# Turning a column vector with VectorE and storing it from ScalarE's queue, in place of a TensorE transpose

## The chip, the core and the metric

The kernel runs on one core of a Trainium2 chip. A core has TensorE (PE: matrix products, and transposes as products with an identity), VectorE (DVE), ScalarE (ACT), GpSimd (POOL) and SyncE (SP), which run side by side and wait for each other through semaphores. DMAs are started by instructions of SP, ACT or POOL and run on 16 DMA engines of the core. The metric is the device time of one execution in microseconds (us). The kernel before took 1218.98 us (median of 3 runs, 1218.74 to 1221.97).

## The reference

Sixteen graphs of 1024 nodes with 256 features go through two layers. `adj` holds only zeros and ones. Cut to what matters:

```python
# layer 0: gated sum over neighbours
e0    = leaky(einsum('bid,bjd->bij', h * a0, h))          # slope 0.2
alpha = sigmoid(where(adj == 1, e0, -max))                # 0 where there is no edge
x     = layernorm(x + einsum('bij,bjd->bid', alpha, h) + bias)
# layer 1: graph attention
Hh    = x @ W
s, d  = Hh @ a[:256], Hh @ a[256:]
e     = where(adj != 0, exp(-leaky(s[:, None] + d[None, :])), 0)
x     = layernorm(x + elu((e @ Hh) / rowsum(e)))
```

Since exp(-leaky(z)) is the smaller of exp(-z) and exp(-0.2 z), the kernel writes it as exp(-0.2 z) times min(1, p q), where p belongs to the row node (from s) and q to the column node (from d). The row's own factor falls out in the division by the row sum, and the column's factor is multiplied into H. What is left of `e` for an edge is min(p q, 1), and for no edge min(p q, 0): one VectorE instruction, min(p q, adj).

## The kernel before, in words

All work is float32. The nodes of one graph are cut into 8 tiles of 128. The main loop runs over b = 1 to 15, and I call one turn a slot. A slot makes layer 0 of graph b and layer 1 of graph b-1 ("prev"), and ends the layer norm of graph b-2 ("done"). A 16th part behind the loop makes layer 1 of the last graph. The order of all instructions is the order of the Python text, engine by engine (`manual_schedule`). Each engine takes its instructions strictly in that order.

A slot starts with the eight score strips jt = 0 to 7 (`strip`, L240): TensorE multiplies (L254) into PSUM tiles, ScalarE takes two tanh (L262, L263), VectorE the larger of them (L264), `finish` (L266) masks it with adj, and POOL adds 2 to the diagonal (`add_twice`, L284). The scores are symmetric, so a strip is made only right of the diagonal. What lies under it is a turned copy: `dump` (L286) turns the strip in squares of 32x32 on VectorE (L290) and stores it in DRAM in four pieces from SP's queue (L294), and `gather` (L296) loads it back into `al` with one DMA (L298). `mask` (L302) then masks it on VectorE (L305). I write dump 3, gather 1 and so on for the strip that they belong to. On SP's queue the order around the change is dump 2, gather 1, dump 3, gather 2, gather 3, dump 4, dump 5, gather 4.

The product of alpha and x is made of seven smaller ones (`product`, L457, and `combine_al`, L449, whose VectorE instructions are L455). Layer 1 of prev runs between: `project` (L567) makes H, and ScalarE writes p into columns 0 to 7 and q into columns 8 to 15 of the tile `pq_kept`, 128 partitions x 32 columns (L594), one column a node tile. After all eight, `share_p` (L606) brings p, which lies down the partitions, into a row that every partition has: the tile `p`, 128 x 1024. `weights` (L637) reads it in L643, and `sum1` (L647) multiplies the result with H (L648).

In `share_p` TensorE turns `pq_kept` (L610) into PSUM, ScalarE copies the 8 x 128 result to the tile `row` (L612), POOL stores it in DRAM as `p_row` (L614, eight rows of 512 bytes), and, when that has landed, loads it back onto all partitions (L616). Only then does POOL go on to `center` (L368) of graph done: L338, L357 to L363, L373 and L374, small instructions on 128 x 8 elements that give the scale of the layer norm. ScalarE's `scale1` (L379) waits for it, and on ScalarE's queue `check_adj` (L130) and `unite(b, "c11")` (L499) stand behind `scale1`. VectorE's `turn_y(b, 1)` (L521) waits for L499, and `weights` 5 to 7 stand behind that.

In the last slot `share_half` (L618) does the same work for half of p at a time and in another way: VectorE turns the whole `pq_kept` in squares of 32x32 (L624). Then p of node tile t lies in row t of each of the four blocks of 32 partitions, and four DMAs from POOL's queue, one a block, store it (L628).

One thing that the text does not show is in the built program. The DMAs of SP and of ACT share eight completion semaphores, given in turn in the order of the program. A DMA waits, before it is issued, until the DMA eight places before it has landed, unless other waits ensure that already. POOL's DMAs have semaphores of their own.

Of the kernel before, what the change touches and what calls it, by code (L numbers as in the profile page):

```python
# [9 lines left out]
F32 = mybir.dt.float32  # L10
# [8 lines left out]
P = 128  # L19
HALF = 512  # L20
BIG = 1.0e30
SLOPE = 0.2
SQ = 32
# [7 lines left out]
def one_kind_pass(  # L31
# [33 lines left out]
    nc = tc.nc  # L65
    B, N, D = x.shape
    NT = N // P
    ND = D // P
    HT = HALF // P
# [6 lines left out]
    one = ctx.enter_context(tc.tile_pool(name="one", bufs=1))  # L76
    two = ctx.enter_context(tc.tile_pool(name="two", bufs=2))
    dram = ctx.enter_context(tc.tile_pool(name="dram", bufs=2, space=bass.MemoryType.DRAM))
    small = ctx.enter_context(tc.tile_pool(name="small", bufs=3))
    ps_e = ctx.enter_context(tc.tile_pool(name="ps_e", bufs=3, space=PSUM))  # L80
    ps_t = ctx.enter_context(tc.tile_pool(name="ps_t", bufs=2, space=PSUM))
# [27 lines left out]
    def adj_rows(b, j0, j1, columns):  # L109

        for g in range(2):
            k0, k1 = max(j0, g * HT), min(j1, (g + 1) * HT)
            if k0 < k1:
                yield slice(k0, k1), adjs[b, g][:, k0 - g * HT : k1 - g * HT, columns]
# [35 lines left out]
    ident = const.tile([P, P], F32, tag="ident", name="ident")  # L150
# [29 lines left out]
    pq_kept = const.tile([P, SQ], F32, tag="pq", name="pq_kept")  # L180
# [121 lines left out]
    def mask(b, t, j0=0, j1=NT):  # L302
        for js, rows in adj_rows(b, max(t + 1, j0), j1, ts(t, P)):
            v = als[b][:, js, ts(t, P)]
            nc.vector.scalar_tensor_tensor(v, v, 1.0, rows, ALU.add, ALU.mult)  # L305
# [143 lines left out]
    def combine_al(b, k, j0, j1):  # L449

        left, right = slice(0, HALF), slice(HALF, N)
        top, low = als[b][:, j0:j1, :], als[b][:, HT + j0 : HT + j1, :]
        t1, m12, m21, m22 = top[:, :, left], top[:, :, right], low[:, :, left], low[:, :, right]
        out_, in0, in1 = {1: (t1, t1, m12), 2: (t1, m21, t1), 3: (m12, t1, m12), 4: (m21, m22, t1)}[k]
        nc.vector.tensor_tensor(out_, in0, in1, ALU.subtract)  # L455

    def product(b, k):  # L457

        left, right = slice(0, HALF), slice(HALF, N)
        top, low = als[b][:, 0:HT, :], als[b][:, HT:, :]  # L460
        x_ = xs[b]
        lhs, rhs = {
            1: (x_[:, 0:HT, 0:P], top[:, :, right]),
            2: (x_[:, HT:, 0:P], low[:, :, right]),
            3: (Ss[b][:, 2, :, :], low[:, :, left]),
            4: (x_[:, HT:, P:D], low[:, :, left]),
            5: (Ss[b][:, 0, :, :], top[:, :, left]),
            6: (Ss[b][:, 1, :, :], top[:, :, left]),
            7: (x_[:, 0:HT, P:D], top[:, :, right]),
        }[k]  # L470
        bank = {1: "Q", 2: "Q", 3: "V", 5: "V", 4: "W", 7: "W", 6: "R"}[k]
        first = k in (1, 5, 6, 7)
        if first:
            pool, tag = {"Q": (ps_t, "t"), "V": (ps_acc, "acc")}.get(bank, (ps_e, "e"))
            banks[bank] = pool.tile([P, HALF], F32, tag=tag, name=f"p{bank}_{b}")
        for jt in range(HT):
            nc.tensor.matmul(  # L477
                banks[bank],
                lhsT=lhs[:, jt, :],
                rhs=rhs[:, jt, :],  # L480
                start=first and jt == 0,
                stop=jt == HT - 1,
                skip_group_check=True,
            )
# [27 lines left out]
    def new_yT(b):  # L512
        yTs[b] = x1Ts[b] = one.tile([P, ND, N], F32, tag="x1T", name=f"yT_{b}")
# [24 lines left out]
    x1Ts, Hs, pqs, p_bcs, es = {}, {}, {}, {}, {}  # L538
# [64 lines left out]
            nc.scalar.mul(H, acc, wr)  # L603
        unscaled.clear()

    def share_p(b):  # L606


        pt = ps_t.tile([P, HT, P], F32, tag="t", name=f"prow_{b}")[0:NT, 0, :]
        nc.tensor.transpose(pt, pq_kept[:, 0:NT], ident)  # L610
        row = one.tile([NT, P], F32, tag="row", name=f"row_{b}")
        nc.scalar.copy(row, pt)  # L612
        p_row = dram.tile([N], F32, tag="p_row", name=f"p_row_{b}")
        nc.gpsimd.dma_start(p_row.rearrange("(t p) -> t p", p=P), row)  # L614
        p_bcs[b] = one.tile([P, N], F32, tag="p", name=f"p_{b}")
        nc.gpsimd.dma_start(p_bcs[b], p_row.partition_broadcast(P))  # L616

    def share_half(b, t0):  # L618


        if t0 == 0:
            p_bcs[b] = one.tile([P, N], F32, tag="p", name=f"p_{b}")
        pT = one.tile([P, SQ], F32, tag="pT", name=f"pT_{b}_{t0}")
        nc.vector.transpose(pT, pq_kept)  # L624
        p_row = dram.tile([HALF], F32, tag="p_half", name=f"p_row_{b}_{t0}")
        v = p_row.rearrange("(t i j) -> i t j", i=P // SQ, j=SQ)
        for i in range(P // SQ):
            nc.gpsimd.dma_start(v[i], pT[ds(i * SQ + t0, HT), :])  # L628
        nc.gpsimd.dma_start(p_bcs[b][:, ds(t0 * P, HALF)], p_row.partition_broadcast(P))

    def check_pq(b):
        near = small.tile([P, 2, NT], F32, tag="near", name=f"near_{b}")
# [80 lines left out]
    def deviation1(b, t):  # L713
        deviation(ys[b][t], mv1s[b][:, t, :])
# [66 lines left out]
    for b in range(1, B):  # L781
        prev, done = b - 1, b - 2
# [6 lines left out]
        for jt in range(NT):  # L789
            if jt == 4:  # L790
                mask(b, 0, 0, HT)
                combine_al(b, 1, 0, 2)
            if jt == 5:
                new_yT(b)
                product(b, 1)
                share_p(prev)
                mask(b, 1, 0, HT)
                combine_al(b, 1, 2, 3)
                mask(b, 0, HT)
                mask(b, 1, HT)  # L800
                mask(b, 2, 0, HT)
                combine_al(b, 1, 3, HT)
                mask(b, 2, HT)
                if done >= 0:
                    r1s[done] = center(mv1s[done], f"1_{done}", unit=1.0 / D)
            if jt == 6:
                unite(b, "p1")
                product(b, 5)
                unite(b, "p5")
                combine_al(b, 2, 0, HT)  # L810
            strip(b, jt)
            if jt == 5:
                mask(b, 3, HT)
            finish(b, jt, ends=False)
            if jt == 4:
                gather(b, 3)
            if jt < NT - 1:
                dump(b, jt)
            if jt < 2 and done >= 0:
                deviation1(done, NT - 2 + jt)  # L820
            if prev == 0 and jt == 0:
                turn_x1(0, 0)
            if prev == 0 and jt == 1:
                transpose_x1(0)
            if jt >= 1 and jt != 4:
                gather(b, jt - 1)
            if jt < 4 and b == 1:
                combine_x(b, jt)
            for t in projects[jt]:
                project(prev, t)  # L830
            if jt == 4:
                evict_H()
            add_twice(b, jt)
# [74 lines left out]
        for t in range(NT):  # L908
            if t >= n_first:
                acc = sum_of(t)  # L910
                for m in range(NT):
                    sum1(prev, t, acc, m)
            if last and t == 7:
                for m in range(4):
                    weights(b, m, 0, HT)
            elu(prev, t, *((first[t], rinvs[t]) if t < n_first else (acc,)))
            if last and t in (2, 3):
                for q in range(HT):
                    stats0(b, (t - 2) * HT + q)
                roots0(b, t - 2)  # L920
            if t >= 1:
                add(prev, t - 1)
            if t >= 2:
                deviation1(prev, t - 2)
            if not last and t in (3, 5):
                sums0(b, (t - 3) // 2)
                if t == 5:
                    load_adj(b + 1, 1, behind=mv0s[b][:, HT, 0:1])
            if not last and t >= 4:
                for q in range(2 * t - 8, 2 * t - 6):  # L930
                    deviation0(b, q)
                if t % 2 == 1:
                    roots0(b, (t - 5) // 2)
            for n in ([0], [1], [2, 3])[t - 5] if not last and t >= 5 else []:
                combine_x(b + 1, n)
            if t == 3 and not last:
                scale_x(b + 1, 0)
                scale_x(b + 1, 1)
            if last and t in (4, 6):
                t0 = (t - 4) // 2 * HT  # L940
                for n in range(HT):
                    project(b, t0 + n)
                evict_H()
                share_half(b, t0)
            if last and t in (5, 7):
                for q in range(HT):
                    scale0(b, (t - 5) // 2 * HT + q)
            if last and t == 7:
                for m in range(4, 6):
                    weights(b, m, 0, HT)  # L950
# [524 lines left out]
```

## Time and profile before

The profiled execution took 1218.96 us, and its span was 1217.2 us (1.76 us lie outside). TensorE's granted clock was 0.998.

| | busy us | share of the span |
|---|---|---|
| TensorE | 1206.9 | 99% |
| VectorE | 993.4 | 82% |
| ScalarE | 846.5 | 70% |
| GpSimd | 391.2 | 32% |
| the 15 transposes of L610, as listed | 15 x 0.273 = 4.1 | 0.3% |
| the 15 copies of L612 | 15 x 0.255 = 3.8 | 0.3% |
| POOL's wait for `p_row` to land (L616) | 40.5 in 15 | 3.3% |

A slot starts with the first product of its strip 0; these starts are at 130.42, 204.84, 279.26, 353.68, 428.10, 502.52, 577.14, 651.56, 726.17, 800.59, 875.87, 950.29, 1024.71 and 1099.43 us in the chain of waits. Their distance is 74.42 us, and longer in the slots from 502.52 (74.62), 651.56 (74.61), 800.59 (75.28) and 1024.71 (74.72). "At +22.4" below means 22.4 us after the start of a slot.

How to read the profile: a line of the timeline has the start in us, the length in us, the engine (SPq is SP's DMA queue), the line of the kernel, the operation, output<-inputs, sizes and the count of merged instructions. In brackets stand the idle time of the engine just before and what ended it. "DMA al<-mir" there means that a DMA landed.

### The profile page before, as it was taken

The page shows a single profiled execution, that of the slowest core. Times are in us where ns is not written, and L with a number is a line of the kernel's source. Part 1 is how long each engine was busy: PE and PEld are TensorE (multiplying, and loading weights), DVE is VectorE, ACT ScalarE, POOL GpSimd, SP SyncE. Part 2 cuts the span into 40 slices and gives each one's busy share as a digit, 9 for nine tenths or more (in the row PEclk, how much of TensorE's full clock was granted, in tenths as well). Part 3 has the DMA queues.
Part 4 walks back from the last instruction along what each step waited for, and adds up shares of the span by engine and source line. Part 5 has one row for each costly group of instructions (what it writes and reads, how often), then busy time and mean ns, then how long its engine had stood idle before and what let it go on. Part 6 is the DMA issues. An engine that isn't in the chain of part 4 may idle for free.

```text
span 1217.2 us, 15868 instructions
## 1 busy us (share of the span) xinstructions
PE 1206.9 (99%) x4400; PEld 819.4 (67%) x4400; DVE 993.4 (82%) x1759; ACT 846.5 (70%) x2150; POOL 391.2 (32%) x730
## 2 busy tenths in 40 slices
PE   9999999999999999999999999999999999999997
PEld 6757657576575866758667585775757657576686
DVE  5698797887969789797897978879798796887957
ACT  4574867767687676867768677786776867577674
POOL 3320333404243142441414324143340433404243
PEclk9999999999999999999999999999999999999999
DMA  9568787797878878788787886877769787887512
GB/s 195 104 133 153 130 158 154 148 184 137 154 152 155 180 136 160 145 166 172 142 171 132 156 179 132 176 139 143 173 143 189 128 156 151 156 182 137 112 52 73
DMA packets 604600, 180.66 MB, mean 148 GB/s; under 512 B 482012, under 2 KB 586968, under 8 KB 604504
## 3 DMA queue, kind: packets, MB, share of 16 engines
q1 hardware_dynamic: 582800, 136.90, 56.0%
q0 software_dynamic: 21008, 42.01, 18.8%
q8 instruction: 37, 0.61, 0.2%
q10 hardware_dynamic: 696, 0.66, 0.2%
q14 instruction: 59, 0.48, 0.1%
HBM read 152.44 MB, written 60.62 MB: 175 GB/s over the span
## 4 chain that ended last, share of the span: by engine, by line
PE 96%; ACT 2%; DVE 1%; POOL 1%; DMA 0%; issue 0%; ACTq 0%; DVEq 0%; POOLq 0%
PE acc L648 36%; PE pe L254 20%; PE pH L582 9%; PE pQ L477 8%; PE pV L477 8%; PE pW L477 8%; PE pR L477 4%; PE acc L396 2%; ACT junk L130 0%; ACT y_kept L379 0%; DMA p_row<-row 0%; PE busy L149 0%; PE pal L313 0%; ACT x L379 0%; POOL ve L338 0%
## 5 line engine op out<-in xcount | busy, mean ns | idle before, releaser
L648 PE MATMUL acc<-H,e 128*128 128x257 f32 x2032 | 445.6, 380 | 0.6 <-DVE e L643 0.6
L648 PEld LDWEIGHTS acc<-H,e 128*128 128x128 f32 x2032 | 384.8, 190 | 64.8 <-issue 7.2
L254 PE MATMUL pe<-xa,xT 128*128 128x384 f32 (+1 forms) x720 | 249.5, 486 | 0.2 <-DVE xa L235 0.2
L254 PEld LDWEIGHTS pe<-xa,xT 128*128 128x128 f32 x720 | 132.8, 190 | 90.0 <-issue 50.7
L284 POOL TENSOR_TENSOR al<-ident,al 128x128 f32<-128x128 f32 x128 | 103.7, 818 | 198.6 <-DVE al L270 198.5
L643 DVE SCALAR_TENSOR_TENSOR e<-p,pq_kept,adj 128x1024 f32<-128x1024 f32 (+1 forms) x136 | 159.2, 1224 | 0.0
L455 DVE TENSOR_TENSOR al<-al 128x1024 f32<-128x1024 f32 (+2 forms) x105 | 144.9, 1380 | 11.7 <-POOL al L284 4.5
L264 DVE TENSOR_TENSOR tb<-tb,low 128x512 f32<-128x512 f32 (+1 forms) x192 | 104.7, 551 | 39.8 <-ACT low L263 39.7
L262 ACT ACTIVATE tb<-pe 128x512 f32<-128x512 f32 (+1 forms) x192 | 93.8, 489 | 59.4 <-PE pe L254 57.7
L130 ACT ACTIVATE junk<-adj,minus 128x2048 bf16<-128x2048 bf16 x64 | 127.3, 1990 | 0.0
L582 PE MATMUL pH<-Wx,yT 128*128 128x258 f32 x480 | 116.3, 380 | 0.0
L104 POOL CAST adj<-x 128x1 bf16<-128x1 f32 x15 | 3.2, 212 | 348.9 <-DMA x<-y_rows 298.4
L582 PEld LDWEIGHTS pH<-Wx,yT 128*128 128x128 f32 x480 | 91.2, 190 | 31.1 <-issue 13.4
L477 PE MATMUL pV<-al,S 128*128 128x512 f32 x240 | 107.9, 592 | 0.0
L477 PE MATMUL pW<-al,x 128*128 128x512 f32 x240 | 107.9, 592 | 0.0
L477 PE MATMUL pQ<-al,x 128*128 128x512 f32 x240 | 107.9, 592 | 0.0
L270 DVE SCALAR_TENSOR_TENSOR al<-tb,adj 128x512 f32<-128x512 f32 (+7 forms) x132 | 97.4, 739 | 4.5
L305 DVE SCALAR_TENSOR_TENSOR al<-al,adj 128x512 f32<-128x512 f32 (+3 forms) x150 | 81.6, 564 | 18.6 <-DMA al<-mir 18.1
L263 ACT ACTIVATE low<-pe 128x512 f32<-128x512 f32 (+1 forms) x192 | 94.1, 490 | 1.2 <-DVE tb L264 1.2
L379 ACT ACTIVATE y_kept<-y_kept,mr,r 128x256 f32<-128x256 f32 x120 | 64.9, 588 | 42.9 <-POOL mr L374 41.7
L674 ACT ACTIVATE sums<-acc,tiny 128x1 f32<-128x1 f32 x45 | 11.7, 261 | 111.0 <-PE acc L648 111.0
L684 DVE TENSOR_SCALAR rinv<-acc 128x1 f32<-128x1 f32 x82 | 12.8, 157 | 89.9 <-PE acc L648 89.8
(152 smaller groups left out, 1681.7 us busy)
## 6 DMA issues: line engine op xcount, KB each, us to landing
adj<-in_adjT POOLq DMA_DIRECT2D x30, 1024.0 KB, 8.4
x<-in_x SPq DMA_DIRECT2D x15, 1024.0 KB
y_rows<-Z SPq DMA_DIRECT2D x240, 64.0 KB, 2.0
x<-y_rows SPq DMA_DIRECT2D x30, 512.0 KB, 4.3
out<-y_kept SPq DMA_DIRECT2D x30, 512.0 KB, 3.0
xT<-in_x SPq DMA_DIRECT2D x112, 128.0 KB, 4.0
p<-p_row POOLq DMA_DIRECT2D x15, 512.0 KB, 4.2
mir<-tb SPq DMA_DIRECT2D x60, 112.0 KB, 3.0
```

The source lines that it names most:

```text
L130: nc.scalar.activation(junk, rows, AF.Square, bias=minus1, scale=2.0, accum_out=chk[:, b * CHECKS + n : b * CHECKS + n + 1],)
L254: nc.tensor.matmul(pe[:, 0:w], lhsT=xTs[b][:, c, ts(jt, P)], rhs=xas[b][:, c, ds(jt * P + o, w)], start=(c == 0), stop=(c == ND - 1),)
L262: nc.scalar.activation(tb[:, ds(o, w)], pe[:, 0:w], AF.Tanh, scale=0.5)
L263: nc.scalar.activation(low[:, 0:w], pe[:, 0:w], AF.Tanh, scale=0.5 * SLOPE)
L264: nc.vector.tensor_tensor(tb[:, ds(o, w)], tb[:, ds(o, w)], low[:, 0:w], ALU.max)
L270: nc.vector.scalar_tensor_tensor(als[b][:, jt, c0:c1], tbs[b, jt][:, c0 - jt * P : c1 - jt * P], 1.0, adjs[b, jt // HT][:, jt % HT, c0:c1] ...
L284: nc.gpsimd.tensor_tensor(diag, ident2, diag, ALU.add)
L455: nc.vector.tensor_tensor(out_, in0, in1, ALU.subtract)
L477: nc.tensor.matmul(banks[bank], lhsT=lhs[:, jt, :], rhs=rhs[:, jt, :], start=first and jt == 0, stop=jt == HT - 1, skip_group_check=True,)
L582: nc.tensor.matmul(pt, lhsT=x1Ts[b][:, c, ts(t, P)], rhs=Wx[:, c, :], start=(c == 0), stop=(c == ND - 1),)
L643: nc.vector.scalar_tensor_tensor(e, p_bcs[b][:, cols], q, rows, ALU.mult, ALU.min)
L648: nc.tensor.matmul(acc, lhsT=es[b][:, m, ts(t, P)], rhs=Hs[b][m], start=(m == 0), stop=(m == NT - 1),)
```

## The change

In the slots `share_p` is replaced by `save_p` and a shorter `share_p`, and the last slot uses the same two functions. VectorE turns `pq_kept` in 32x32 squares (128 x 32) into the tile `pT`, and four DMAs store p: from ScalarE's queue in the slots, from POOL's queue, as before, in the last one. POOL then loads the row onto all partitions, as before. TensorE's transpose and ScalarE's copy are gone from the slots. On VectorE the transpose stands behind `mask(b, 1, 0, HT)`, which the call was in front of before.

```diff
-    def share_p(b):
-        pt = ps_t.tile([P, HT, P], F32, tag="t", name=f"prow_{b}")[0:NT, 0, :]
-        nc.tensor.transpose(pt, pq_kept[:, 0:NT], ident)
-        row = one.tile([NT, P], F32, tag="row", name=f"row_{b}")
-        nc.scalar.copy(row, pt)
-        p_row = dram.tile([N], F32, tag="p_row", name=f"p_row_{b}")
-        nc.gpsimd.dma_start(p_row.rearrange("(t p) -> t p", p=P), row)
-        p_bcs[b] = one.tile([P, N], F32, tag="p", name=f"p_{b}")
-        nc.gpsimd.dma_start(p_bcs[b], p_row.partition_broadcast(P))
-
-    def share_half(b, t0):
+    p_rows = {}
+
+    def save_p(b, t0, n, queue):
+        pT = one.tile([P, SQ], F32, tag="pT", name=f"pT_{b}_{t0}")
+        nc.vector.transpose(pT, pq_kept)
+        p_rows[b, t0] = dram.tile([n * P], F32, tag=f"p_row_{n}", name=f"p_row_{b}_{t0}")
+        v = p_rows[b, t0].rearrange("(t i j) -> i t j", i=P // SQ, j=SQ)
+        for i in range(P // SQ):
+            queue.dma_start(v[i], pT[ds(i * SQ + t0, n), :])
+
+    def share_p(b, t0, n):
         if t0 == 0:
             p_bcs[b] = one.tile([P, N], F32, tag="p", name=f"p_{b}")
...
-        nc.gpsimd.dma_start(p_bcs[b][:, ds(t0 * P, HALF)], p_row.partition_broadcast(P))
+        nc.gpsimd.dma_start(
+            p_bcs[b][:, ds(t0 * P, n * P)], p_rows[b, t0].partition_broadcast(P)
+        )
...
             if jt == 5:
                 new_yT(b)
                 product(b, 1)
-                share_p(prev)
                 mask(b, 1, 0, HT)
+                save_p(prev, 0, NT, nc.scalar)
+                share_p(prev, 0, NT)
                 combine_al(b, 1, 2, 3)
...
-                share_half(b, t0)
+                save_p(b, t0, HT, nc.gpsimd)
+                share_p(b, t0, HT)
```

In the built program the four new DMAs of a slot are numbered, for the eight semaphores, among the four pieces of dump 3: two of them behind its second piece and two behind its third.

More of the change, by code (lines that the diff above doesn't have):

```diff
@@ L604, in evict_H @@
         unscaled.clear()
-    def share_p(b):
-        pt = ps_t.tile([P, HT, P], F32, tag="t", name=f"prow_{b}")[0:NT, 0, :]
-        nc.tensor.transpose(pt, pq_kept[:, 0:NT], ident)
-        row = one.tile([NT, P], F32, tag="row", name=f"row_{b}")
-        nc.scalar.copy(row, pt)
-        p_row = dram.tile([N], F32, tag="p_row", name=f"p_row_{b}")
-        nc.gpsimd.dma_start(p_row.rearrange("(t p) -> t p", p=P), row)
-        p_bcs[b] = one.tile([P, N], F32, tag="p", name=f"p_{b}")
-        nc.gpsimd.dma_start(p_bcs[b], p_row.partition_broadcast(P))
-    def share_half(b, t0):
+    p_rows = {}
[7 more added lines that the diff above has]
+    def share_p(b, t0, n):
         if t0 == 0:
             p_bcs[b] = one.tile([P, N], F32, tag="p", name=f"p_{b}")
[L623 to L628, printed above, removed]
-        nc.gpsimd.dma_start(p_bcs[b][:, ds(t0 * P, HALF)], p_row.partition_broadcast(P))
+        nc.gpsimd.dma_start(
+            p_bcs[b][:, ds(t0 * P, n * P)], p_rows[b, t0].partition_broadcast(P)
+        )
     def check_pq(b):
```

## The prediction

> **What bounds the kernel now.** I first read the busy times and the chain that ended last, then the instructions on the tile of the transpose, then a slot's timeline, engine by engine.
>
> ```profile
> PE 1206.9 (99%) x4400; PEld 819.4 (67%) x4400; DVE 993.4 (82%) x1759; ACT 846.5 (70%) x2150; POOL 391.2 (32%) x730
> PE 96%; ACT 2%; DVE 1%; POOL 1%; DMA 0%; issue 0%; ACTq 0%; DVEq 0%; POOLq 0%
> L610 PE MATMUL prow<-ident,pq_kept x15: 272/273/273, 79.1 to 1122.6; 128*8 128x128 f32 x15
> 522.38 3.43 PE pQ L477 x8
> 525.82 0.11 PE prow L610
> 525.93 1.29 PE pe L254 x4
> ```
>
> TensorE is the bound: 99% busy, 96% of the chain. The next two facts size the change. The transpose is listed with 0.273 us, but the chain gives it 0.11 us; matmuls are pipelined, and the next product starts 0.107 us after it (128 of 512 columns that take 0.429). So a transpose is worth 0.107 us.
>
> The second fact is that VectorE is a close second bound, by way of POOL and of the gathers. Two slots, one from 428.10 and one from 502.52, differ:
>
> ```profile
> 455.50 0.57 POOL L616 DMA_DIRECT2D p<-p_row  x1 [2.79 <-DMA p_row<-row]
> 456.60 1.67 POOL L357 TENSOR_TENSOR r<-ve,power 128x8 f32<-128x8 f32 x1
> 456.86 2.25 DVE L455 TENSOR_TENSOR al<-al 128x2048 f32<-128x2048 f32 x1
> ...
> 529.88 0.56 POOL L616 DMA_DIRECT2D p<-p_row  x1 [2.74 <-DMA p_row<-row]
> 530.80 3.72 POOL L357 TENSOR_TENSOR r<-ve,power 128x8 f32<-128x8 f32 x1
> ...
> 530.71 2.27 DVE L455 TENSOR_TENSOR al<-al 128x2048 f32<-128x2048 f32 x1
> 553.10 1.25 DVE L521 STREAM_TRANSPOSE Z<-yT 128x1024 f32<-128x1024 f32 x1 [0.64 <-ACT yT L499]
> 554.27 3.63 DVE L643 SCALAR_TENSOR_TENSOR e<-p,pq_kept,adj 128x1024 f32<-128x1024 f32 x3
> ```
>
> In the first slot POOL's L357 starts before VectorE's large combine (L455, 2048 elements) and takes 1.67; in the second it starts 0.09 after it and takes 3.72, the combine's length more. POOL's chain then ends at +37.0 instead of +32.8, ScalarE's scalings start that late, VectorE waits 0.64 for L499, and `weights` 5 ends at +52.96, where TensorE needs it (sixth group of `sum1`: +46.45 and 15 products of 0.4345 make +52.97). That slot is 0.20 longer. Over all slots, L616 has to start about 0.95 before the large combine; in four it doesn't, and these are the long ones: 0.20 + 0.19 + 0.86 + 0.30 = 1.55 us.
>
> The third view is SP's queue and VectorE's waits for gathers, in the same stretches.
>
> ```profile
> 520.75 0.45 SPq L298 DMA_DIRECT2D al<-mir  x1
> 521.24 2.23 SPq L294 DMA_DIRECT2D mir<-tb  x4
> 523.58 2.56 SPq L298 DMA_DIRECT2D al<-mir  x2
> ...
> 453.23 0.29 DVE L305 SCALAR_TENSOR_TENSOR al<-al,adj 128x128 f32<-128x128 f32 x1 [0.31 <-DMA al<-mir]
> al<-mir SPq DMA_DIRECT2D x15, 384.0 KB, 3.7
> al<-mir SPq DMA_DIRECT2D x15, 320.0 KB, 3.4
> ```
>
> Gather 1 (384 KB), the four pieces of dump 3, and gathers 2 (320 KB) and 3 leave SP in that order. In the slot from 428.10 VectorE waits 0.31 for gather 2: the masks have no room for a later gather. Where gather 2 is waited for, the large combine starts 3.66 after its landing, and `weights` 5 ends 23.23 after that start.
>
> **The change, part by part.**
>
> 1. *Removed on TensorE*: 15 x 0.107 = 1.6 us, all on the path. Its weight load lies beside the product before and costs nothing.
>
> 2. *Removed on ScalarE and POOL*: 15 copies of 0.255 and 15 issues of 0.63. Neither engine is on the path there (ScalarE idles 1.85 before the copy, POOL 2.74 after the issue), so they are worth what they do to POOL's chain (5).
>
> 3. *Added on VectorE*: 15 transposes of 128x32, 0.21 each by the two of L624 in the last slot, 3.2 us. The next mask waits for gather 2 (4), and that wait hides them. Without that cover VectorE ends up to 0.21 later; its room in the slot from 428.10 is 52.76 - 51.99 = 0.8 (52.76 is where a `weights` 5 would be just early enough by the long slot), so nothing is due.
>
> 4. *Added waits on the DMA queues*: this is the dear part. The built program deals eight semaphores to the DMAs of SP and ACT together. With four new DMAs numbered among the pieces of dump 3, the DMA eight places before the last piece is no longer dump 2's first but gather 1. So SP stops until gather 1 has landed, and behind it stand gathers 2 and 3. Gather 1 is issued at +18.0 to +18.8 and lands 3.4 to 4.1 later, at +21.6 to +22.9, mean +22.2. The last piece left at +20.6 until now. It now goes at +22.2, takes 0.3 (SP's issues behind an idle time do), and gather 2 goes at about +22.6 in place of +21.4, never before dump 3's first piece has landed (mean +22.5). How long gather 2 then takes is in no row. Bounds: 2.8, the fastest gather 3 (256 KB, with little queued ahead), and 3.6, the slowest gather 2 of now. I take 3.15, between gather 3's usual 3.0 and gather 2's 3.36, for the queue ahead of it will be shorter. It lands at +25.75, against +24.8. The large combine starts 3.66 later, at +29.4, and `weights` 5 ends at +52.65. TensorE, 0.107 earlier, needs it by 52.76 - 0.107 = +52.65. So it is a tie, and what slots lose beyond it counts. Slot by slot, with each slot's landing of gather 1 and of dump 3's first piece: 0.15, 0.66, 0.07, 0.07, 0.51, 0.06 and eight times nothing, 1.5 us in all. With 2.8 it is 0.5, with 3.6 it is 6.0. Gather 3 waits for that last piece (about 2.2 after its issue), lands near +27.5, and its mask is due at +27.9: no more. Dump 4's pieces and dump 5's first now wait for the new DMAs to land, by about +27; dump 4 stands behind gather 3 anyway, and dump 5 is due at +29.4. Gathers 4 to 6 come 1.2 later and have 1.5 and more of room before their masks.
>
> 5. *POOL's chain*. The turned tile is ready 0.65 after the start of mask 1 (mean +22.4), at +23.05. ScalarE's four issues cost between 0.24 (the second DMA of its queue) and 0.57 (its first): 1.0 to 2.3. Landing takes between 1.5 (16 KB pieces of dump 6, p in the last slot 1.6) and 3.1 (`p_row` now). So L616 starts between +25.5 and +28.4, middle +26.9; now it is +27.4. The large combine is at +29.4, so the whole range lies 0.95 or more ahead of it, no slot is late in the old way, and the 1.55 us go. The load of p has 10 us until `weights` 0.
>
> 6. *ScalarE stands for it*. Its queue now waits for VectorE's transpose instead of TensorE's, and behind the wait are the tanhs of strip 5 (ready +24.7), whose L264 on VectorE comes at +25.6 to +27.0 now and later then. The four issues end at +24.1 to +25.4. At worst the tanhs are 0.7 late, end at +26.2, and gather 2's wait has VectorE busy until +27.3 before L264. Cost nothing; without the wait for gather 2 the upper end would cost VectorE 0.3.
>
> Sum: -1.6 - 1.55 + 1.5 = -1.65. The profiled execution took 1218.96, and the median of the runs is 1218.98, so that both give **1217.3 us**. With the ends of (4): 1216.3 to 1221.8.
>
> [...]
>
> **Rivals.**
>
> *The gathers pass unhurt* (12%). If gather 2 takes 2.8 or less, VectorE is in time and the whole gain stays: 1218.96 - 3.15 = 1215.8. For it: gather 2 has to wait for a full queue now. Against it: its 320 KB.
>
> *The wait for gather 1 becomes the bound* (28%), the slower side. Its place is SP's last piece of dump 3, its price each 0.1 us of gather 2 beyond +25.75, in 14 slots, 1.4 us. A landing at +26.0 on average eats the gain; at +26.45 the stalls are 0.7 a slot, 9.8 in all, 1225.6 us. For it: VectorE waits for gathers already, product 5's fourth part needs the combine behind gather 2 by +27.0, and the landing of a gather varies by 0.7. Against: at the longest landing so far it is 1221.8.
>
> *POOL stays late* (8%). If ScalarE's issues cost what the slower of SP's do (1.05 each), L616 starts at +23.05 + 4.2 + 2.3 = +29.6, after the combine; each slot is then like the one from 800.59 (0.86): -1.6 - 1.55 + 14 x 0.86 = +8.9, 1227.9 us. Against: ScalarE's own issues never took more than 0.57.
>
> *The path isn't relieved* (in the likeliest case's range): if the long slots come back by another way, only 1.6 are gained, 1217.4.
>
> **How the numbers follow.** The likeliest case, a tie at gather 2, has 52%. What a measurement can tell of this kernel is about 0.3%, 3.7 us: 1215.3 and 1222.6. Faster than that needs more than the whole gain of 3.2; I give it 10%, half of the first rival and a little of the likeliest. Slower: two thirds of the second rival, all of the third, and a little of the likeliest, 30%. The rest, 60%, is no difference. The range from 1215.2 to 1224.5 leaves out 18%: the upper part of the second rival, the third, and a little at the lower end. The likeliest case's own range is 1216.2 to 1220.
>
> **What would show it.** The transposes of L610 gone, and 0.107 less between the product before and strip 5. On SP's queue, the last piece of dump 3 at +22.2 with 1.5 us of idle time before it, and gather 2 at +22.6. On VectorE, a wait for `al<-mir` of 0.5 to 1.2 before the third mask of jt = 5 in every slot. On POOL, L616 near +26.9 and L357 never over 2 us. ScalarE's waits for `mr` (L379) all near 2 and none of 6. Slots of 74.31, and some longer. I am wrong if gather 2 still leaves at +21.4, if POOL starts later than the combine, or if slots are longer by another wait, such as product 5 for VectorE's combine.

## The result, and the profile after

The changed kernel takes 1220.22 us (median of 22 runs, 1218.29 to 1222.08), the kernel before 1218.51 in the same comparison (22 runs, 1217.49 to 1221.97). The ratio is 1.0014, with a 95% interval of 1.0007 to 1.0020: 1.7 us slower, where I had forecast 1.7 faster. Both lie within the 0.3% that I called no difference, and the range held the time; the sign is wrong, and the interval shows it.

The profiled execution took 1221.67 us, its span is 1219.9. The busy times and the chain that ended last, on the page of the changed kernel:

```profile
PE 1208.1 (99%) x4385; PEld 820.6 (67%) x4385; DVE 993.7 (81%) x1774; ACT 842.8 (69%) x2135; POOL 385.5 (32%) x715
PE 95%; DMA 2%; DVE 1%; ACT 1%; SPq 0%; issue 0%; ACTq 0%; DVEq 0%
```

The chain has 2% of DMA, which was 0%. The first two parts of the change did what was forecast. In the chain of waits of the slot from 505.90 strip 5 follows product 4 with no transpose between, and POOL's L357 takes 1.86 us and starts before VectorE's large combine, where it took 3.72 in the late slot from 502.52 of the kernel before (timeline, POOL and VectorE of the same slot):

```profile
525.77 3.43 PE pQ L477 x8
529.20 1.29 PE pe L254 x4
```

```profile
532.62 0.64 POOL L621 DMA_DIRECT2D p<-p_row  x1 [4.50 <-DMA p_row<-pT]
534.09 1.86 POOL L357 TENSOR_TENSOR r<-ve,power 128x8 f32<-128x8 f32 x1
...
534.82 2.25 DVE L455 TENSOR_TENSOR al<-al 128x2048 f32<-128x2048 f32 x1
```

That slot takes 74.31 us, 0.11 less than the usual one before. What is lost is in the chain of the slot from 207.46. Its columns are start, length, engine and work:

```profile
224.40 1.64 SPq L294
226.05 0.05 issue
226.10 0.03 SPq L298
226.13 0.04 issue
226.16 3.94 DMA al<-mir
230.10 0.02 issue
230.12 0.30 SPq L294
...
230.53 0.03 SPq L298
230.56 0.03 issue
230.59 3.28 DMA al<-mir
...
233.89 0.30 DVE al L305
...
234.28 0.70 DVE al L455
...
235.03 1.12 PE pV L477 x2
```

Read from above: gather 1 is issued at 226.10 and lands at 230.10. Only then SP issues the last piece of dump 3 (L294, 0.30), and behind it gather 2, which lands at 233.87. VectorE masks it (L305), combines one tile (L455), and only then TensorE goes on with the fourth part of product 5. The timeline lists 0.41 us of idle time on TensorE there; against a slot that nothing delays, what follows starts 0.69 later, and `sum1` loses another 0.24 where it waits for `weights`, so the slot takes 75.24. The waits of the whole run tell the same. Columns: us in total, times, the longest. The first fence is of the kernel before (VectorE), the second of the changed one (SP, VectorE):

```profile
DVE al L305 <- DMA al<-mir: 18.1, 18, 1.6
...
DVE al L455 <- POOL al L284: 4.5, 4, 1.1
```

```profile
SPq L294 <- DMA al<-mir: 19.1, 15, 1.7
...
DVE al L305 <- DMA al<-mir: 30.9, 31, 1.6
```

SP stands 1.27 us a slot for gather 1, VectorE 12.8 us longer in all for gathers, and the four waits of the old late slots are gone. The trace also has the number of each DMA's semaphore: eight numbers for all DMAs of SP and ScalarE, and eight others for POOL's, in both kernels. In the changed one, in all 14 slots, the last piece of dump 3 has the same one as gather 1, eight places before it, and in the kernel before it has the same one as the first piece of dump 2.

The spans of five profiles, cut into four parts, tell where the time is. "Again" are second profiles of the two kernels (e5 and e6 below), "one store" is the fastest kernel found (e7). The start is that of the first slot in TensorE's timeline, 0.16 before the chain's; "first slot" is the first of the starts listed ahead of the prediction, that of b = 2, and the turn b = 1 lies before it. Spans are given to 0.1, so the ends are good to 0.05.

| us | before | before again | changed | changed again | one store |
|---|---|---|---|---|---|
| to the first slot | 130.26 | 130.35 | 132.22 | 130.27 | 130.18 |
| the 13 distances from there to the last slot | 969.01 | 967.83 | 968.41 | 969.09 | 965.99 |
| last slot to the issue of the last output store | 114.37 | 114.34 | 114.49 | 114.66 | 114.26 |
| from there to the end | 3.56 | 3.28 | 4.78 | 4.98 | 3.57 |
| span | 1217.2 | 1215.8 | 1219.9 | 1219.0 | 1214.0 |

Thirteen slots of 74.31 are 966.0. So the changed kernel loses 2.4 and 3.1 us there and 0.2 and 0.4 in the last slot, to late gathers. The start of the first profile was chance. The end is 1.2 to 1.7 us longer in both profiles, and nothing in the prediction speaks of it.

### The profile page after: what moved, and what is told of

Its sections match the earlier page's. It is cut to its first block, busy times and chain, and to the rows that moved or that the text cites. A ratio compares the mean times of both kernels' runs of the same rounds, so it can differ in the third digit from the quotient of the medians.

```text
span 1219.9 us, 15900 instructions
## 1 busy us (share of the span) xinstructions
PE 1208.1 (99%) x4385; PEld 820.6 (67%) x4385; DVE 993.7 (81%) x1774; ACT 842.8 (69%) x2135; POOL 385.5 (32%) x715
## 4 chain that ended last, share of the span: by engine, by line
PE 95%; DMA 2%; DVE 1%; ACT 1%; SPq 0%; issue 0%; ACTq 0%; DVEq 0%
PE acc L642 36%; PE pe L254 19%; PE pW L477 8%; PE pH L582 8%; PE pV L477 8%; PE pQ L477 8%; PE pR L477 4%; PE acc L396 2%; DMA al<-mir 1%; SPq L294 0%; DMA mir<-tb 0%; DMA x<-in_x 0%; PE pal L313 0%; PE pxT L230 0%; DVE al L270 0%
## 5 line engine op out<-in xcount | busy, mean ns | idle before, releaser
L284 POOL TENSOR_TENSOR al<-ident,al 128x128 f32<-128x128 f32 x128 | 111.5, 879 | 201.7 <-DVE al L270 201.6
L455 DVE TENSOR_TENSOR al<-al 128x1024 f32<-128x1024 f32 (+2 forms) x105 | 143.7, 1369 | 5.1
L305 DVE SCALAR_TENSOR_TENSOR al<-al,adj 128x512 f32<-128x512 f32 (+3 forms) x150 | 83.1, 570 | 30.9 <-DMA al<-mir 30.9
L477 PEld LDWEIGHTS pW<-al,x 128*128 128x128 f32 x240 | 45.5, 190 | 57.5 <-issue 55.3
```

What stands on the lines that cost most here:

```text
L284: nc.gpsimd.tensor_tensor(diag, ident2, diag, ALU.add)
L477: nc.tensor.matmul(banks[bank], lhsT=lhs[:, jt, :], rhs=rhs[:, jt, :], start=first and jt == 0, stop=jt == HT - 1, skip_group_check=True,)
```

## The experiments

Three theories stood at the beginning. **G**: gather 2 is held up behind the last piece of dump 3, which waits for gather 1, because the four new DMAs shift the dealing of the eight semaphores. **Q**: ScalarE, or VectorE's transpose, stands on the path. **S**: the loss is at the start and the end, and the slots don't matter. A fourth one, **L**, came up on the way. All ratios are to the kernel before on the same chip.

### Fewer stores on ScalarE's queue

POOL's DMAs have eight semaphores of their own in both traces, so a store that moves to POOL's queue takes one number out. e1 moves two, e2 one:

```diff
         for i in range(P // SQ):
-            queue.dma_start(v[i], pT[ds(i * SQ + t0, n), :])
+            q = nc.gpsimd if i >= 2 else queue      # e2: i == 3
+            q.dma_start(v[i], pT[ds(i * SQ + t0, n), :])
```

> The changed kernel, but only two of the four stores of p leave from ScalarE's queue, and the other two from POOL's. In the built program the last piece of dump 3 then waits for dump 2's third piece, as harmless as before the change, and no longer for gather 1. Theory G (the loss comes from gather 2, held up behind that piece): gather 2 leaves at +21.4 again, VectorE's waits for gathers fall from 0.65 to 1.5 in each slot to 0.3 in a few, product 5 never stands, all slots are 74.3, and the time is about 3 us under the kernel before, ratio 0.997 to 0.9985. Rival Q (ScalarE stands for VectorE's transpose and the issues behind it): the wait stays, two issues less, ratio 1.000 to 1.0014. Rival S (the loss lies ahead of the slots and behind them, where the profile of the changed kernel is 2.0 and 1.2 us longer): ratio about 1.001, with slots at 74.3 and the start still at +2 us.

Measured: 1216.45 us (1215.32 to 1217.88), ratio 0.9984 (0.9975 to 0.9993), span 1215.4. All slots are 74.31 but the first (74.44) and the last, which is 0.4 longer than in the kernel with one store. SP waits for gather 1 nowhere.

> The changed kernel with three stores from ScalarE's queue and one from POOL's. The last piece of dump 3 waits for dump 2's last piece, which has landed by then; but gather 2 itself now waits for gather 1. Theory G: gather 2 leaves as gather 1 lands, +22.2, between the +21.4 of before and the +22.5 of the changed kernel; stalls at product 5 shrink from 2.7 us in the profiled execution to about 1, the ratio lies between those of two and four stores, 0.998 to 1.000. Rival Q: ratio 1.000 to 1.0014, like four. Rival S: 1.001.

Measured: 1216.36 us (1215.88 to 1218.85), ratio 0.9985 (0.9976 to 0.9994), span 1214.6, all slots 74.31. Here the number of gather 2 itself comes eight after gather 1, so SP does wait, one place later in its queue (waits of SP):

```profile
SPq L298 <- DMA al<-mir: 10.1, 15, 1.0
```

That is 0.67 us a slot in place of 1.27, and VectorE's mask of gather 2 starts at +24.6 to +25.7, +25.1 in the mean. TensorE stands in those slots of the changed kernel where that mask starts after about +25.75. So half the wait (0.67 a slot) cost nothing, and the whole one (1.27) cost about 3 us: for this kernel it is a threshold. In both kernels ScalarE still waits for VectorE's transpose and VectorE still makes it; Q falls.

The third kernel moves all four stores to POOL's queue, so that SP's numbering is the old one:

```diff
-                save_p(prev, 0, NT, nc.scalar)
+                save_p(prev, 0, NT, nc.gpsimd)
```

> The changed kernel with all four stores from POOL's queue. SP's queue is dealt its semaphores exactly as in the kernel before, ScalarE neither waits nor issues. POOL issues four of 0.51 in place of one of 0.63, so the load of p (L621) starts near +27.7, about where a slot's POOL chain is late or not. Theory G: gathers as before, no stall at product 5; -1.6 of TensorE for certain, and the late slots of POOL's chain stay in some slots, up to 1.5 us or somewhat more; ratio 0.997 to 0.9995. Rival Q: the same or lower. Rival S: about 1.001.

Measured: 1223.97 us (1222.22 to 1224.85), ratio 1.0046 (1.0033 to 1.0060). The expectation missed. SP's waits for gather 1 are gone as expected, but POOL now issues five DMAs itself and comes late. Timeline of the slot from 876.66, POOL first and then VectorE:

```profile
899.76 2.18 POOL L615 DMA_DIRECT2D p_row<-pT  x4 [0.80 <-DVE pT L611]
904.49 0.57 POOL L621 DMA_DIRECT2D p<-p_row  x1 [2.55 <-DMA p_row<-pT]
905.13 2.07 POOL L338 TENSOR_SCALAR ve<-mv 128x8 f32<-128x8 f32 x1
907.28 1.72 POOL L357 TENSOR_TENSOR r<-ve,power 128x8 f32<-128x8 f32 x1
...
904.88 2.25 DVE L455 TENSOR_TENSOR al<-al 128x2048 f32<-128x2048 f32 x1
914.11 1.47 DVE L455 TENSOR_TENSOR al<-al 128x1024 f32<-128x1024 f32 x1 [1.12 <-POOL al L284]
927.25 1.25 DVE L521 STREAM_TRANSPOSE Z<-yT 128x1024 f32<-128x1024 f32 x1 [0.64 <-ACT yT L499]
```

The load of p (L621) starts 0.39 before the large combine, where the prediction asks for 0.95; L338 runs beside the combine and takes 2.07 (0.40 in the slot from 130.42 of the kernel before), L357 starts behind it, and the two old marks of a late slot are back, the wait for L284 and the one for L499 (0.64, as in the late slot before). Eleven of the 13 slots that can be measured from start to start are longer than 74.31, up to 75.06. It is the rival "POOL stays late" of the prediction, by POOL's issues (0.52 each, 2.18 for four) instead of ScalarE's (0.31 each). The slots lose 4.0 us against 74.31 in this profile, the fastest of the five runs, and the end of the span is about 1.4 longer than in the kernel before (below). So one or two of the stores can leave from POOL's queue (e2, e1), but not all four.

### The stores alone

e4 is the kernel before with VectorE's transpose and four stores on ScalarE's queue added; nobody reads them, and p comes by the old way:

```diff
                 mask(b, 1, 0, HT)
+                save_p(prev, 0, NT, nc.scalar)   # share_p(prev) stays as it was
```

> The kernel before, and in addition VectorE's transpose and the four stores from ScalarE's queue at their new place; nobody reads what they store, and p goes the old way, by TensorE, ScalarE and POOL. SP's queue waits as in the changed kernel. Theory G: gather 2 leaves at +22.5, VectorE waits for it in each slot, stalls at product 5 as in the changed kernel or 0.1 more a slot, TensorE keeps its 15 x 0.107: about 1.6 to 3 us over the changed kernel, ratio 1.002 to 1.004. POOL's chain is not late any more, as VectorE's large combine comes 0.9 later. Rival Q: ScalarE's copy and the stores both stand in its queue: ratio 1.003 to 1.006. Rival S: about 1.003 too.

Measured: 1220.27 us (1218.97 to 1223.15), ratio 1.0017 (1.0008 to 1.0026), a little under the 1.002 to 1.004 expected. Its slots are up to 76.04, with TensorE standing 0.05 to 1.36 at product 5 in six of them (the profiled run, 1223.0 us, is one of the slowest), and SP has the changed kernel's wait:

```profile
SPq L294 <- DMA al<-mir: 20.3, 15, 1.8
```

The added stores bring the stalls with them without any other part of the change.

### Both kernels again

> The changed kernel as it is, for a second profile. Theory G (gather 2 is held up behind the last piece of dump 3): about 1220.2 us, ratio 1.0005 to 1.0025; slots of 74.31 where gather 2 lands before +25.75, longer ones where it lands later, 2 to 4 us of stalls in all, at the fourth part of product 5; the first slot starts near 130.7, as in the other profiles, so that the 2 us by which it started later in the first profile were chance. Rival S (the change makes the start longer): the first slot starts near 132.3 again.

Measured: 1219.93 us (1218.89 to 1222.61), ratio 1.0011 (1.0002 to 1.0020). The first slot starts at 130.27: the late start was chance. The stalls are there again, 3.5 us with the last slot, the longest in the slots from 205.45 (1.39), 801.54 (0.75) and 130.43 (0.71), each with gather 2 landing at +26.4 or later. The end was 4.98 again.

> The kernel before as it is, for a second profile. If the late slots of POOL's chain (1.55 us in the first profile) come in every execution, there are some four again, and 1.3 to 1.8 us in them; then two and three stores on ScalarE's queue should have gained 3.15 and something else takes 1.2 us of it. If they come by chance, there are fewer, 0 to 0.8 us in them, and the 1.9 us that two and three stores gained are about the 1.6 of TensorE's transposes and the rest.

Measured: 1217.82 us (1217.67 to 1219.25), ratio 0.9992 (0.9983 to 1.0001). Two slots are long, by 0.19 and 0.17, not four by 1.55, and neither is late in the old way: VectorE waits neither for L284 nor for L499 in this profile, and in these two slots it is the mask of gather 2 that starts late, at +25.9 and +26.0. So the late slots of POOL's chain come by chance: four in the first profile, none in this one.

### One store

VectorE's transpose turns the whole 128x32 tile. e7 writes all of it, 16 KB, in one DMA from ScalarE's queue; the first 4 KB in DRAM are p, the rest is not read. The numbering shifts by one:

```diff
+        if n == NT:
+            whole = dram.tile([SQ * P], F32, tag="p_whole", name=f"p_row_{b}_{t0}")
+            p_rows[b, t0] = whole[0 : n * P]
+            queue.dma_start(whole.rearrange("(t i j) -> i t j", i=P // SQ, j=SQ), pT)
+            return
```

> The turned p is written with one store of 16 KB (the whole 128x32 tile, of which the first 4 KB in DRAM are p) on ScalarE's queue, in place of four. Theory G: the numbering shifts by one; the last piece of dump 3 then waits for the second piece of dump 2, which has long landed, gather 2 leaves near +21.4 as in the kernel before and lands by +25.2; no slot is longer than 74.35, and the time is 1215.8 to 1217.0, ratio 0.998 to 0.999. Rival Q (ScalarE, or VectorE's transpose, standing on the path): those are as in the changed kernel, so 1219 to 1221. A rival on the store itself: 128 pieces of 128 bytes in one transfer land later than the four did, L616 starts after +29, and POOL's chain is late: 1220 to 1228.

Measured: 1216.23 us (1215.87 to 1218.84), ratio 0.9988 (0.9979 to 0.9997), span 1214.0. Every slot is 74.31. SP's queue in the slot from 204.65 goes through dump 3 without a stop, gather 2 leaves at +21.72 (the changed kernel's left at +21.88 to +23.31):

```profile
223.99 2.29 SPq L294 DMA_DIRECT2D mir<-tb  x4
226.37 2.48 SPq L298 DMA_DIRECT2D al<-mir  x2
```

One issue on ScalarE (0.53) also brings p earlier: POOL's load starts at +25.1 to +26.5 there, +26.4 to +27.6 in the changed kernel. A second comparison:

> The kernel with one store of 16 KB as it is, for a second profile and a second comparison: ratio 0.9975 to 0.999, all slots 74.31 but for one or two, and the end 3.3 to 3.8 us behind the last output store, as in its first profile.

Measured: 1216.43 us (1215.85 to 1218.51), ratio 0.9984 (0.9975 to 0.9993); one slot of 74.72, all others 74.31, end 3.5. This is a version that beats both kernels: by the medians it is 2.5 and 1.8 us under the kernel before in the two comparisons (by the ratios 1.5 and 1.9), and 3.7 under the changed one (1219.93 in the first of them). That the pieces in DRAM are 128 bytes shows no price here: from the store's issue at 227.9 to POOL's load at 230.5 are 2.6 us in this slot, issue and landing together; with the rows of 512 bytes from POOL's queue they are 3.3 in the slot from 130.42 of the kernel before (154.41 to 157.75).

### The largest dose

e8 asks for the transpose and its four stores one line earlier, ahead of the mask of gather 1. The operations are the same, but the stores are now numbered among the pieces of dump 2, and so pieces of dump 3 and gathers 2 and 3 are those that wait, for the stores themselves:

```diff
                 product(b, 1)
-                mask(b, 1, 0, HT)
                 save_p(prev, 0, NT, nc.scalar)
                 share_p(prev, 0, NT)
+                mask(b, 1, 0, HT)
```

> The same operations as the changed kernel, with the transpose and its four stores asked for ahead of the first mask of jt = 5, so that p is written earlier. The stores are then numbered among the pieces of dump 2, and it is gather 2 that has the number eight after the second of them, gather 3 that of the third, a piece of dump 3 that of the first. Theory G: gather 2 cannot leave before a store has landed, about +24 to +25, and lands near +28; each slot is 2 to 3 us longer, 28 to 42 us in all, 1246 to 1260 us. If p's own lateness or ScalarE's standing set the time (rival Q): p is earlier by 0.3 to 0.7, and the time is that of the changed kernel or less, 1216 to 1220.

Measured: 1275.14 us (1272.67 to 1276.01), ratio 1.0459 (1.0443 to 1.0475): 56 us over the kernel before, G's direction, and more than its 28 to 42 us. The chain of the slot from 290.4 shows why:

```profile
313.23 0.10 DVE pT L611
313.33 0.02 issue
313.35 1.14 DMA p_row<-pT
314.50 0.02 issue
314.51 0.30 SPq L294
314.82 0.04 issue
314.86 2.00 DMA mir<-tb
316.87 0.02 SPq L298
...
316.98 5.68 DMA al<-mir
322.66 0.02 issue
322.68 0.70 DVE al L305
```

A piece of dump 3 waits for a store of p, gather 3 for that piece, VectorE's mask for gather 3: the third gather is late too, which I had not counted. Gather 2 lands near +28, as expected, and TensorE idles 1.6 to 3.1 us a slot for it; in eight slots it idles another 0.8 to 2.0 us for the mask of gather 3. POOL gets p earlier here (+25.2 to +26.4, +25.5 in the mean against +26.9), and that is of no use.

### The price of TensorE's transpose

e9 and e10 put the transpose back where it was, read by nobody, into the kernel with one store and into the changed one. It runs in all 15 turns of the loop, not in 14 as the two expectations say:

```diff
                 share_p(prev, 0, NT)
+                pt = ps_t.tile([P, HT, P], F32, tag="t", name=f"prow_{prev}")[0:NT, 0, :]
+                nc.tensor.transpose(pt, pq_kept[:, 0:NT], ident)
```

> The kernel with one store of 16 KB, with TensorE's transpose put back in its old place, 14 times, its result read by nobody. Where no gather is late, the slot is TensorE's: 0.107 more in each, 74.42 in place of 74.31, +1.5 us, 1217.7 us, ratio to the kernel before about 0.9995. A rival by the listed duration of 0.273 us: +3.8 us, 1220.0. If TensorE has slack after all: 1216.2.

Measured: 1217.95 us (1217.56 to 1218.51), ratio 0.9997 (0.9988 to 1.0006), against 1216.43 for the kernel with one store in the same comparison: 1.52 us for 15, 0.10 each, and all slots 74.42, 0.11 more than without it. The listed 0.273 would have been 4.1.

> The changed kernel with TensorE's transpose put back, 14 times, its result read by nobody. Theory G: in the slots that wait for gather 2 the 0.107 is hidden (the gather's landing sets the slot, and TensorE waits that much less), in the others it counts, so +0.6 to +1.5 us, 1220.7 to 1221.7 us, ratio 1.002 to 1.0028, as for the kernel before with four unread stores (1.0017). It is also a second program with the changed kernel's queues for the time between the last output store and the end, which was 4.8 and 5.0 us in the two profiles of the changed kernel and 3.3 to 3.8 in the kernel before and in those with two, three and one stores: if the change makes it longer, it is near 4.9 here too; if it goes by how the program lies, it can be near 3.5.

Measured: 1221.08 us (1219.58 to 1222.58), ratio 1.0022 (1.0013 to 1.0031): about 1 us for the same 15 transposes, since slots that wait for gather 2 hide them. Its end is 4.66.

### The end

The time from the last output store's issue to the end of the span parts the kernels without a middle: 3.28 to 3.8 in eight profiles (before twice, e1, e2, e4, e7, e9, e11), 4.66 to 4.98 in five (changed twice, e3, e8, e10). Numbering, POOL, TensorE and VectorE don't part them so: e4 and e10 have the same number of instructions on all of TensorE, VectorE, POOL and SP in the built program, and ends of 3.8 and 4.66. ScalarE's number does. It is 3836, 3837, 3852 and 3896 in those with the short end, 3867 in the changed kernel, e8 and e10, and 3807 in e3. So theory L: the end goes by how ScalarE's program lies. e12 and e13 add copies of one column on ScalarE, which nobody reads, to the changed kernel (3899 then) and to the one with one store (3869). There are 32 of them, two in each of the 15 turns and two more in the first, where the expectations say 30:

```diff
             add_twice(b, jt)
+            if jt == 2 or (jt == 3 and b == 1):
+                spare = one.tile([P, 2], F32, tag="spare", name=f"spare_{b}_{jt}")
+                for k in range(2):
+                    nc.scalar.copy(spare[:, ds(k, 1)], ident[:, ds(k, 1)])
```

> The changed kernel with 30 copies of one column added on ScalarE (two in each slot, at a place where it idles, and two more in the first), read by nobody, and nothing else. ScalarE's program is then 32 instructions longer, about as long as in the kernel before with four unread stores, whose end is short. Theory L (the 1.3 us behind the last output store go by the length of ScalarE's program, that is by how it lies): the end is 3.3 to 3.9 us in place of 4.7 to 5.0, and the time is 0.9 to 1.4 us less than the changed kernel's, 1218.7 to 1219.3, ratio to the kernel before 1.000 to 1.001; the slots keep their 2 to 3.5 us of stalls. Rival (the way p is stored makes the end long): the end stays at 4.7 to 5.0 and the time at 1220 to 1220.5.

Measured: 1218.73 us (1217.88 to 1220.30), ratio 1.0001 (0.9992 to 1.0010).

> The kernel with one store of 16 KB, with the same 30 unread copies on ScalarE. Its ScalarE program is then as long as the changed kernel's but for two instructions. Theory L: its end becomes long, 4.7 to 5.0 us, and its time 1217.4 to 1217.9 in place of 1216.3, although no gather is late and all slots are 74.31. Rival: the end stays at 3.5 and the time at 1216.2 to 1216.5.

Measured: 1218.42 us (1217.65 to 1220.48), ratio 0.9999 (0.9990 to 1.0008), with all slots 74.30.

The last output store in SP's timeline, for the changed kernel, then with the copies (e12), then for one store and for one store with the copies (e13); their spans are 1219.9, 1217.4, 1214.0 and 1215.9 us:

```profile
1215.12 0.37 SPq L1433 DMA_DIRECT2D out<-y_last  x1
```

```profile
1213.76 0.37 SPq L1437 DMA_DIRECT2D out<-y_last  x1
```

```profile
1210.43 0.37 SPq L1438 DMA_DIRECT2D out<-y_last  x1
```

```profile
1210.23 0.37 SPq L1442 DMA_DIRECT2D out<-y_last  x1
```

The ends are 4.78, 3.64, 3.57 and 5.67 us. More work on ScalarE made the changed kernel 1.2 to 1.5 us faster and the one with one store 2.0 to 2.2 slower by the medians, and the slots of e12 keep their stalls (2.3 us and 0.7 in the last). Both went the way that L says; the end of 5.67 and the 1218.42 us of e13 are more than it expected.

The closing instructions show where this time goes. Behind the last store all engines wait for each other twice. ScalarE takes part each time with a DRAIN and an EVENT_SEMAPHORE, the last four instructions of its program. The rows of its two DRAINs, for the changed kernel, e12 and e13, have the shortest, median and longest in ns, then the starts of the first and the second in us:

```profile
L1467 ACTq DRAIN  x2: 8/72/135, 1217.5 to 1219.5; - x2
```

```profile
L1471 ACTq DRAIN  x2: 8/8/8, 1216.0 to 1216.8; - x2
```

```profile
L1476 ACTq DRAIN  x2: 8/72/136, 1214.9 to 1215.3; - x2
```

In e12 each DRAIN starts 0.07 us behind the instruction before it, as in all profiles with the short end. In the changed kernel the second one starts 1.29 behind (1.52 in the second profile, 1.34 in e8, 1.24 in e10), and in e13 the first one 2.41 behind; the trace shows nothing that it waits for. In the built programs the late DRAIN is in all five profiles the 3866th of ScalarE's instructions: the last but one of 3867, and the last but three of 3869. So in these five profiles the stall is at one place, counted from the start of ScalarE's program, and the added copies moved the program's end onto that place (e13) or off it (e12). In e13 it comes ahead of both rounds of waiting, which is why that end is the longest.

e3 is another case, and its 3807 instructions have no part in it: ScalarE shows 0.07 twice. There POOL ends last: its first closing DRAIN takes 4.23 us, where it takes 2.27 in the changed kernel (the rows of POOL's DRAINs, changed kernel and e3):

```profile
L1467 POOLq DRAIN  x3: 46/107/2273, 1214.4 to 1218.6; - x3
```

```profile
L1467 POOLq DRAIN  x3: 46/107/4233, 1215.4 to 1220.1; - x3
```

In these runs this time goes with the stores of p that POOL issued in the whole run: 2.27 us with 8, 2.68 with 23 (the kernel before, e2, e4), 3.09 with 38 (e1) and 4.23 with 68 (e3). Only in e3 does it make the end late.

So the changed kernel's long end comes from ScalarE's closing instructions and not from the way p travels: e12 has the same stores and the short end, e13 has one store and the longest. Why ScalarE stands at that place is not settled, and no profile here shows it.

## Why the prediction was right and wrong

Two steps failed. The stalls behind gather 2, 1.5 us in part 4, measured 2.7 to 3.5. And the sum had no term for the end of the span, which put 1.2 to 1.7 on top. With them the forecast gain of 1.7 us became a loss of 1.7.

*TensorE's 1.6 us* (part 1): right, 1.52 by e9, 0.10 each. In the changed kernel the late slots hide some of it: about 1 us is left there (e10).

*ScalarE and POOL are worth nothing themselves, VectorE's transposes are hidden, ScalarE may stand* (2, 3, 6): right. ScalarE's four issues took 1.36 in the slot from 132.38 where I had 1.0 to 2.3, and the kernels without stalls have the transposes too.

*The DMA queues* (4): the mechanism was right, to the piece, and so were the means. Gather 2 left at +22.5 on average in the first profile (forecast +22.6), and its mask started at +25.73 (forecast landing +25.75, and a stall from there on). What was mis-sized is the term that I called 1.5 us: it measured 2.7, 3.5 and 3.0 (the changed kernel twice, e12). I had taken each slot's landing of gather 1 from the one profile of before, and one landing time of 3.15 for gather 2. Both vary from slot to slot and from run to run: gather 1 took 3.3 to 4.7, gather 2 3.0 to 3.4 where it was late (once 4.1), and its mask started anywhere between +25.1 and +26.9. With the mean on the threshold, the spread alone makes the cost. I also named the wrong place: nearly all of it is lost at the fourth part of product 5, the place of the second rival, and at `weights` only 0.2 in one slot of each of the two profiles. The rival had the place and the threshold right, and its price of 0.7 a slot was too high: it is 0.2 on average.

*POOL's chain* (5): the load of p (L616, now L621) starts at +26.9 on average (forecast +26.9), L357 never takes over 2.0, and ScalarE's waits for POOL fell from a longest of 6.7 to 2.8. The bound of 0.95 is not a sharp one: in the kernel before, the load starts 0.96 ahead of the combine in the late slot from 1024.71 and 0.94 ahead in the slot from 353.68, which is not late. But the 1.55 us that this was to give back were counted from one profiled execution, and the second profile of before has nothing of them. Against the profiled execution the term is right; against the median it is too large.

*What the sum did not have*: the end, 1.2 to 1.7 us in the profiles, 1.2 to 1.5 between the medians of the changed kernel and of e12. It is the stall of ScalarE's second closing DRAIN, 1.29 and 1.52 us. Without it the changed kernel is level with the one before (1.0001): 1.5 us from TensorE gained, and what an execution has of POOL's late slots (0 and 1.55 in two profiles), and about 3 lost to gather 2. So of the 3.4 us between the change that I forecast (-1.7) and the one measured (+1.7), about 1.4 are the end and 1.2 to 2.0 the stalls. The rest, 0 to 0.8, fits that other executions of before have fewer late slots than its first profile; for that there is one second profile.

## What to carry to other kernels

A DMA added on one queue can delay another queue that never touches its data: with four unread stores on ScalarE's queue SP waited 20.3 us in 15 turns for gather 1 (e4), because the DMAs of both are dealt the same eight semaphores in turn. Where a program deals them so, count which DMA is eight places before each one behind the new ones, and if a wait falls on a load, try fewer and larger DMAs: here one store of 16 KB did what four small ones did, and every slot was 74.31 (e7). Where a forecast lands on a threshold, cost the spread of the landing times and not their mean, and take a stall that occurs by chance in the profile at less than its full size. Before a gain or loss of about a microsecond is put down to a mechanism, look at the start and the end of the span as well, since 32 unread copies moved this kernel by about 1.4 us one way and the one with one store by about 2.1 the other.

## What I had not expected of the hardware

In these runs the end of the span goes with the length of ScalarE's program. In the five profiles in which a closing DRAIN is its 3866th instruction, this DRAIN starts 1.2 to 2.4 us behind the instruction before it, and 0.07 in the others; the end is then 4.7 to 5.0 or 5.7 us behind the last store's issue in place of 3.3 to 3.8, the same in two profiles of one program to within 0.3. And the issues of four small stores took POOL 2.18 us (e3) where they took ScalarE 1.36, and eleven of 13 slots were longer; POOL's DRAIN at the end took 4.23 us with 68 such stores and 2.27 with 8.
